# Three pairs of a phase: the 64-row convolution products replaced by a tap on ScalarE and one on VectorE, and a recurrence cut at five eighths

## The chip, the cores and the metric

The kernel runs on one NeuronCore of one Trainium2 chip. The metric is the device time of one execution in microseconds (us), the median of several runs. Engines are named as in the profile: PE (TensorE, the matrix engine), PEld (its weight loads), DVE (VectorE), ACT (ScalarE), POOL (GpSimd) and SP (SyncE, which here only issues DMAs).

## The reference

Four images of 128 channels, 96 x 96. Each is normalised in groups and read as four sequences of 9216 positions (by rows, by columns, and both backwards). Each sequence goes through the same block, and the four results are joined by a 1x1 product and added to the input:

```python
t = grouped1x1(x, in_proj_w, in_proj_b)            # 128 -> 2*256 channels
u, gate = t[:, :256], t[:, 256:]
u = silu(u)
u = depthwise_conv1d(u, dw_w, taps=5)              # along the sequence
s = ssm_in_w @ u                                   # 32 rows
a = 0.999 + 0.0009 * sigmoid(ssm_delta_w @ u + ..) # 32 rows
bb, cc = tanh(ssm_b_w @ u + ..), tanh(ssm_c_w @ u + ..)
h = exp(prefix) * cumsum(bb * s * exp(-prefix))    # h[l] = a[l] * h[l-1] + bb[l] * s[l]
u = u + ssm_out_w @ (cc * h + ssm_d * s)
y = out_proj_w @ grouped1x1(u * sigmoid(gate), mix_w, mix_b)
out = x + fuse_w @ concat(four y) + fuse_b
```

## The kernel before, in words

Everything is float32. The work is cut into 8 phases (4 images, each first in column order, "V", then in row order, "H"; the phases are numbered 0 to 7, V even, H odd). A phase runs two sequences of one image side by side, s = 0 forward and s = 1 backward. It has 6 steps of 1536 positions, and each step is cut into 4 by position modulo 4: the residues p are taken in the order `TURN` = 1, 2, 3, 0. One residue of both sequences is a *pair*; there are 24 pairs in a phase and 192 in all. This text numbers the pairs of a phase as *places* 0 to 23; place modulo 4 gives the pair of the step (0: p = 1, 1: p = 2, 2: p = 3, 3: p = 0).

The 256 channels of `u` lie in two halves of 128. The five taps of the convolution of the second half are made by ACT (tap 0, `first_tap`, L742) and DVE (taps 1 to 4, `taps`, L744). For the first half the channels of four neighbouring positions are spread over 128 rows of the tile `sil`, so that one residue's five taps fall on two column offsets. `conv` multiplies the 128 rows by banded weights (`band`, 4 taps or 3), and what is left lies at the other offset:

- residues 0 and 3 (`alone`): one tap is left. `add_lone` (L691, one DVE instruction) reads that tap's rows, gathered by DMA into `lone`, and adds tap times weight to the product in PSUM while it writes `u`.
- residues 1 and 2: two taps are left, in 64 rows. `conv_less` adds 8 products with weights `less` (64 rows, 32 columns) to the same PSUM bank, and ACT then copies the bank to `u` (`copy_u`, L717).

Up to place 7 and from place 20 on, the pair also computes the input projection of the step ahead (`front`). From place 8 to 19 the front is not needed, since the second half of a phase reads the kept `sil` of the first half backwards; these pairs have the banks (6, 7) of PSUM for `conv`, and most of them make the gates of a later pair instead (`gate`, then `tanh_one` and `tanh_into`, L593 and L599; `tanh_into` reads banks 6 and 7). Steps 2, 3 and 4 (places 8 to 19) are the steps with gates.

A pair in these steps issues on PE, in this order: `conv`, the output product of an older unit (`accumulate`, weights `w_fin`), `conv_less` if it has one, a second `accumulate`, gates (L557) and `out_of` (the ssm output, L577), then `proj` (weights `main`). ACT runs, from the second half of a pair: tanh of two gates (L593), the next pair's tap 0 (L742), tanh of the other two gates from banks 6 and 7 (L599), then what `proj` needs (L781, L784, L790). The recurrence of a whole step, 1536 positions, is one DVE scan cut in two halves of 768 columns (`scan`, L819): part 0 in the first pair of the next step, part 1 in its second pair. The multiplications that use it are on POOL (`outputs`, L825, L826, L828), as are the additions to the output image (`accumulate`, L879).

The program order on each engine is written out by hand; only the semaphores are put in by the framework. SP issues all DMAs in order: the kept gates (L1066, `kept`), kept `sil` tiles (L513), `lone` (L682), gate inputs (L323), input chunks for the statistics of the next image (`xs`, L437, three buffers) and others.

Of the kernel before, what the change touches and what calls it, by code (L numbers as in the profile page):

```python
# [47 lines left out]
P = 128  # L48
# [20 lines left out]
def conv_preact_kernel(  # L69
# [63 lines left out]

    gmeans = wp.tile([P, 2, P], F32, name="gmean")
    gmean = gmeans[:, 0, :]
    per = DIM // GN_GROUPS
# [11 lines left out]
    for e in range(2):  # L148
        nc.gpsimd.tensor_copy(gmeans[:, 1, bass.ts(e, 64)], gmeans[:, 0, bass.ts(1 - e, 64)])
    gmask = wp.tile([P, 4], F32, name="gmask")  # L150
# [25 lines left out]
    def stats_first(b):  # L176
        mv = sp.tile([P, 2], F32, tag="mv", name=f"mv_{b}")
        nc.vector.bn_aggr(mv, stats[b].rearrange("p c s -> p (c s)"))
        yield
        pm = bank(free[0])  # L180
        product(pm[:, 0:1], gmean, mv[:, 0:1])
        mean = sp.tile([P, 1], F32, tag="mean", name=f"mean_{b}")
        nc.vector.tensor_copy(mean, pm[:, 0:1])
        dev = sp.tile([P, 1], F32, tag="dev", name=f"dev_{b}")
        nc.vector.tensor_sub(dev, mv[:, 0:1], mean)
        ex = sp.tile([P, 1], F32, tag="ex", name=f"ex_{b}")
        nc.vector.scalar_tensor_tensor(ex, dev, dev, mv[:, 1:2], ALU.mult, ALU.add)
        gm4 = sp.tile([P, 4], F32, tag="gm4", name=f"gm4_{b}")
        nc.vector.tensor_scalar_mul(gm4, gmask, mean)
        yield  # L190
        pv = bank(free[0])
        for e in range(2):
            product(pv[:, e : e + 1], gmeans[:, e, :], ex)
# [144 lines left out]

    rp = ctx.enter_context(tc.tile_pool(name="shared", bufs=1))

    def shared():
        return rp.tile([P, 16 * P], F32, tag="shared", name="shared")

    b0 = phases[0][0]
# [6 lines left out]
    load_x([(0, 1), (1, 1), (2, 1), (3, 2), (5, 2), (7, 3), (10, 4), (14, 4), (18, 4), (22, 2)])  # L351
    w_out_fuse = shared()
    nc.sync.dma_start(w_out_fuse[:, 0 : 2 * HID + 4 * P], fuse)
# [8 lines left out]
    d_sb, b_mix, b_out, b_fuse = (w_small[:, a:b] for a, b in ((79, 80), (80, 82), (82, 83), (83, 84)))  # L362
    w_edge = w_small[:, 84:86]
    w_out = w_out_fuse[:, 0:HID]
# [8 lines left out]
    def less_of(p):  # L373
        return 1 if p < 2 else 0

    def less_rows(s, p):
# [4 lines left out]
    less = wp.tile([P, R, 4, 32], F32, name="less")  # L381
    w_fin = wp.tile([P, 4, 2, P], F32, name="w_fin")
    b_fin = wp.tile([P, 1], F32, name="b_fin")
    id32 = wp.tile([P, 32], F32, name="id32")
    ident = w_out_fuse[:, 2 * HID + 4 * P : 2 * HID + 5 * P]
# [4 lines left out]
    for s in range(2):  # L390
        for p in range(R):
            for k in range(2):
                r, to = slice(0, P), band[:, s, p]
                if k == less_of(p):
                    r, to = less_rows(s, p), less[:, p]
                m = R * k - p + R - 1
# [34 lines left out]
    def load_chunks(t):  # L431
        ahead = chunks_of(t - 1) + chunks_of(t) + chunks_of(t + 1)
        for b, c in ahead:
            if (b, c) not in loaded and len(chunks) < 3:
                loaded.add((b, c))
                chunks[b, c] = wk.tile([P, SC], F32, tag="xs", bufs=3, name=f"xs_{b}_{c}")
                nc.sync.dma_start(chunks[b, c], xr[b, :, bass.ts(c, SC)])  # L437
# [222 lines left out]
    def alone(p):  # L660
        return p in (0, R - 1)

# [3 lines left out]
    ]  # L666
    lone = {}

# [15 lines left out]
    def add_lone(i, banks):  # L684
# [4 lines left out]
        else:  # L689
# [10 lines left out]
    def conv_less(i, banks, copy=True):  # L700
        step, p = units[i]["step"], units[i]["p"]
        sil, k, b0 = blocks(step), less_of(p), min(banks)
        for g in range(4):
            for s in range(2):
                r = less_rows(s, p)
                mm(bank(b0 + s), g, less[r, p, g, :], columns(step, sil[s][r, g, :], k),
                   False, True)
# [11 lines left out]
    def less_both(i, banks):  # L719
        step, p = units[i]["step"], units[i]["p"]  # L720
        sil, k = blocks(step), less_of(p)
        for g in range(4):
            for s in range(2):
                r = less_rows(s, p)
                mm(bank(banks[s]), g, less[r, p, g, :], columns(step, sil[s][r, g, :], k), False, True)

# [180 lines left out]
    def head_banks(t):  # L907

        return PROJ if t % 2 or t >= LAG else FRONT[1::-1]

    early = [None]

# [42 lines left out]
    def pair_on(t):  # L955
# [3 lines left out]
        un = units[i]  # L959
        single = alone(un["p"])  # L960
        step, g = divmod(t + R, R)
# [27 lines left out]
        taps(i, range(1, K))  # L989
        conv(i, banks, single)  # L990
        if single:
# [57 lines left out]
        if gated is not None:  # L1049
            if gated % NP > 2:  # L1050
                both = to[:, :, 0]
            else:
                spot = 2 - shift
                both = to[:, spot : spot + 2]
            tanh_into(gated, both, 0, psum[:, 6:8, :N])
        if un["order"] == "V" and un["b"] + 1 < B and un["st"] == NS - 1 and k == R - 1:
# [7 lines left out]
        if gated is not None:  # L1064
            if gated % NP > 2:
                nc.sync.dma_start(keep(gated), to)  # L1066
            else:
                nc.sync.dma_start(keep(gated)[:, :, 0], both)
        load_kept(n + 2)
# [307 lines left out]
```

## Time and profile before

| | us |
|---|---|
| median of 3 runs (lowest, highest) | 1737.48 (1737.05, 1737.89) |
| span of the profiled execution | 1735.2 |
| PE busy | 1713.6 (99%) |
| DVE busy | 1507.9 (87%) |
| ACT busy | 1494.8 (86%) |
| POOL busy | 1447.0 (83%) |
| the 64-row products (`less`), busy in all | 84.1, in 96 pairs |

The span runs from the first instruction to the last. The profiled execution's own time is not recorded apart from it; the median lies 2.3 us above the span, which is what lies around it. The granted TensorE clock is 1.000 all through. In rows of the timeline a number is the start in us, the next is how long the group lasted, and brackets tell how long the engine sat idle before it and what ended that. The page counts each float32 product as two MATMUL records.

### The profile page before, as it was taken

How to read it: one execution, taken by the hardware profiler on the slowest of the kernel's cores; microseconds unless marked ns; L12 is line 12 of the kernel's file. 1: busy time of each engine (PE TensorE's matmuls, PEld its weight loads, DVE VectorE, ACT ScalarE, POOL GpSimd, SP SyncE). 2: the span in 40 equal slices, each digit the busy share in tenths (PEclk: the TensorE clock that was granted, in tenths of full speed). 3: DMA queues.
4: the chain of work that ended last, by engine and by line, in shares of the span. 5: the costliest groups of instructions: out<-in, count | busy, mean ns of one | idle time of the engine just before them, and what ended most of it. 6: DMA issues, size and time to landing. Idle time of an engine off the chain costs nothing.

```text
span 1735.2 us, 54226 instructions
## 1 busy us (share of the span) xinstructions
PE 1713.6 (99%) x22522; PEld 644.7 (37%) x22522; DVE 1507.9 (87%) x1508; ACT 1494.8 (86%) x2544; POOL 1447.0 (83%) x1490
## 2 busy tenths in 40 slices
PE   7999999999999999999999999999999999999998
PEld 4333333343333433344333443334333333333333
DVE  6899998888889998888889999888888888888887
ACT  4888988889888888888988888888998889888875
POOL 3689889888789988888788988887878889887887
PEclk9999999999999999999999999999999999999999
DMA  7746865358884786337896487433887548643364
GB/s 244 235 147 218 288 202 151 124 206 280 275 287 139 262 267 194 118 126 263 260 308 226 150 300 251 144 123 132 294 294 239 179 144 304 201 137 133 147 226 166
DMA packets 154644, 363.66 MB, mean 210 GB/s; under 512 B 19104, under 2 KB 120864, under 8 KB 154400
## 3 DMA queue, kind: packets, MB, share of 16 engines
q1 hardware_dynamic: 154256, 360.16, 62.8%
q8 instruction: 178, 2.92, 0.7%
q14 instruction: 66, 0.54, 0.1%
q10 hardware_dynamic: 144, 0.04, 0.0%
HBM read 221.41 MB, written 138.53 MB: 207 GB/s over the span
## 4 chain that ended last, share of the span: by engine, by line
PE 95%; DVE 2%; ACT 1%; DMA 1%; issue 0%; SPq 0%; DVEq 0%; ACTq 0%
PE psum L130 81%; PE psum L577 8%; PE psum L557 5%; DVE psum L744 1%; PE psum L1188 0%; DMA acc<-in_xr 0%; DMA kept<-shared 0%; DVE u L638 0%; ACT psum L589 0%; ACT psum L742 0%; DVE u L744 0%; ACT sil L527 0%; SPq L335 0%; PE psum L1195 0%; DVE u L691 0%
## 5 line engine op out<-in xcount | busy, mean ns | idle before, releaser
L744 DVE SCALAR_TENSOR_TENSOR psum<-sil,small,psum 128x768 f32<-128x768 f32 x576 | 589.1, 1023 | 42.2 <-ACT psum L742 16.8
L130 PE MATMUL psum<-u,w_fin 128*32 128x384 f32 (+1 forms) x6192 | 541.3, 484 | 1.1 <-ACT ys L860 0.4
L130 PE MATMUL psum<-u,main 128*32 128x384 f32 x6144 | 535.0, 489 | 0.5 <-DVE u L691 0.4
L638 DVE SCALAR_TENSOR_TENSOR u<-gate,psum 128x768 f32<-128x768 f32 x376 | 341.7, 950 | 150.0 <-PE psum L577 50.8
L879 POOL TENSOR_TENSOR acc<-ys,acc 128x384 f32<-128x384 f32 x375 | 411.8, 1120 | 14.0 <-ACT ys L860 1.9
L825 POOL TENSOR_TENSOR t<-t,t 64x384 f32<-64x384 f32 (+1 forms) x192 | 287.2, 1496 | 70.6 <-DVE t L819 48.3
L589 ACT COPY psum<-u 128x768 f32<-128x768 f32 x384 | 301.4, 799 | 10.5 <-DVE u L638 4.3
L130 PEld LDWEIGHTS psum<-u,w_fin 128*32 128x32 f32 x6192 | 195.2, 109 | 309.6 <-issue 235.5
L130 PEld LDWEIGHTS psum<-u,main 128*32 128x32 f32 x6144 | 180.0, 109 | 324.5 <-issue 218.3
L130 PE MATMUL psum<-sil,band 128*32 128x384 f32 x3072 | 285.3, 488 | 0.0
L792 POOL TENSOR_SCALAR t<-tm 64x384 f32<-64x384 f32 x184 | 170.8, 928 | 114.4 <-ACT tm L781 102.4
L826 POOL TENSOR_TENSOR t<-t,t 64x384 f32<-64x384 f32 (+1 forms) x192 | 233.9, 1218 | 15.1
L793 POOL TENSOR_TENSOR t<-t,tm 64x384 f32<-64x384 f32 x192 | 213.8, 1113 | 30.2 <-ACT t L784 15.5
L577 PE MATMUL psum<-t,main 32*128 32x384 f32 x1536 | 228.1, 525 | 4.2 <-ACT psum L589 4.2
L742 ACT ACTIVATE psum<-sil,small 128x768 f32<-128x768 f32 x191 | 172.6, 904 | 65.2 <-DVE u L638 61.9
L744 DVE SCALAR_TENSOR_TENSOR u<-sil,small,psum 128x768 f32<-128x768 f32 x192 | 194.9, 1015 | 6.8
L527 ACT ACTIVATE sil<-psum,bnorm 128x385 f32<-128x385 f32 x384 | 191.6, 584 | 4.0 <-DMA edge<-sil 0.9
L557 PE MATMUL psum<-x_in,wn 32*128 32x384 f32 x768 | 161.7, 498 | 0.0
L862 ACT COPY ys<-psum 128x384 f32<-128x384 f32 x288 | 132.3, 478 | 33.0 <-PE psum L130 28.3
L130 PEld LDWEIGHTS psum<-sil,band 128*32 128x32 f32 x3072 | 88.8, 108 | 171.4 <-issue 63.1
L781 ACT ACTIVATE tm<-psum,small 128x384 f32<-128x384 f32 x192 | 110.9, 578 | 14.0 <-PE psum L130 2.3
L577 PEld LDWEIGHTS psum<-t,main 32*128 32x128 f32 x1536 | 93.9, 183 | 73.7 <-issue 41.0
(108 smaller groups left out, 1512.3 us busy)
## 6 DMA issues: line engine op xcount, KB each, us to landing
gate<-kept SPq DMA_DIRECT2D x114, 768.0 KB, 5.2
kept<-gate SPq DMA_DIRECT2D x74, 768.0 KB, 3.7
sil<-sil SPq DMA_DIRECT2D x64, 770.0 KB, 6.6
lone<-edge SPq DMA_DIRECT2D x40, 770.0 KB, 7.5
x_in<-in_xs SPq DMA_DIRECT2D x250, 96.2 KB, 3.3
edge<-sil SPq DMA_DIRECT2D x96, 192.5 KB, 3.6
out<-acc SPq DMA_DIRECT2D x46, 384.0 KB, 6.4
acc<-in_xr SPq DMA_DIRECT2D x39, 384.0 KB, 6.4
```

Of the source, the lines that this page charges most:

```text
L130: nc.tensor.matmul(o[r, : rhs.shape[-1]], lhsT, rhs, start=start, stop=stop, skip_group_check=True)
L527: nc.scalar.activation(sils[step][:, s, j, g, :], bank(bk)[:, : N + 1], AF.Silu, bias=bn[:, 1:2] if j else bn[:, 4 + g : 5 + g],)
L557: nc.tensor.matmul(bank(to)[:, :N], stats[un["b"]][0][r, s, :], x_in[s][r, q, off : off + N], start=True, stop=True)
L577: nc.tensor.matmul(bank(ssm(bi, s) + j)[:, :N], w_so[r, bass.ts(j, P)], z[r, :], start=(bi, s) not in seeded, stop=True, skip_group_check= ...
L589: nc.scalar.copy(psum[:, ssm(bi, s) : ssm(bi, s) + 2, :N], us[bi][:, s])
L638: nc.vector.scalar_tensor_tensor(v, g, 1.0, pz, ALU.add, ALU.mult)
L742: nc.scalar.activation(part, src, AF.Copy, scale=w_tap[:, 0:1])
L744: nc.vector.scalar_tensor_tensor(us[i][:, :, 1, :] if k == K - 1 else part, src, w_tap[:, k : k + 1], part, ALU.mult, ALU.add,)
L793: nc.gpsimd.tensor_mul(ta[0:64, p, :], tb[0:64, :], tm[0:64, :])
L825: engine.tensor_mul(ta[0:64, p, r], tb[64:P, r], ta[64:P, p, r])
L826: engine.tensor_add(tb[0:64, r], ta[0:64, p, r], tb[0:64, r])
L879: adder.tensor_add(part, y, part)
```

## The change

In the second pair of each step with gates (places 9, 13 and 17; `paired`; 24 pairs in all) the 8 products of `conv_less` go. Their two taps are made elsewhere:

- `seed`: one ACT instruction writes tap 1 times its weight into banks 6 and 7 of PSUM, and `conv` adds to it (`onto`) where it used to overwrite. It stands at the end of the pair before (places 8, 12 and 16), right behind `tanh_into`. It reads a new tile, `middle`.
- `add_lone`, as in a pair with one tap left, makes the other tap and writes `u`, so `copy_u` goes too.
- `copy_middle`: `middle` is filled by 8 DMAs per step of 32 rows x 385 columns, issued by SP (`middles`): four in the third pair of the step before, two in its fourth, two in the first pair of the step itself.

The recurrence is cut at 5/8: part 0 has 960 columns, part 1 has 576 (in all steps but the last). To make room in SBUF, `xs` has two buffers for three, `less` holds two residues for four, and `id32` and the second averaging matrix move into the `shared` tile. `less` is no longer built for residues 0 and 3.

On ACT, around places 8 and 9 of phase 0, where `tm_2_1` is the tanh of `proj` at place 8 and `u_2_2` is what place 9 writes. Before:

```order
L742 ACTIVATE psum<-sil_747,small 128x2x384 [waits DVE_49]
L599 ACTIVATE gate_177<-psum,bnorm_272 128x2x384
L781 ACTIVATE tm_2_1_0_1150<-psum,small 128x384 [waits PE_49,Pool_49]
L784 COPY t_0_2_1_0_1133<-psum 64x384 [waits PE_49]
L790 ACTIVATE t_0_2_1_0_1133<-psum,small 64x384
```

After, in the same place (the names' last numbers and the lines differ):

```order
L765 ACTIVATE psum<-sil_740,small 128x2x384 [waits DVE_49]
L604 ACTIVATE gate_172<-psum,bnorm_267 128x2x384
L662 ACTIVATE psum<-middle_897,small 128x2x384 [waits DMAHW5_49,DMAHW6_49,DMAHW4_49,DMAHW7_49,DMAHW3_49,Activation_49]
L804 ACTIVATE tm_2_1_0_1153<-psum,small 128x384 [waits PE_49,Pool_49]
L807 COPY t_0_2_1_0_1136<-psum 64x384 [waits PE_49]
```

The seed (L662) stands between the tanh of banks 6 and 7 and the tanh of `proj`; it waits for the DMAs that fill `middle` and for ACT's own instruction ahead of it.

On PE, from the end of `proj` of place 8 to the gates of place 9, phase 0. Before:

```order
L130 MATMUL psum<-u_2_1_0_1064,main 32x384 x3
L130 MATMUL psum<-u_2_1_0_1064,main 32x384 [waits Activation_49]
L130 MATMUL psum<-u_2_1_0_1064,main 32x384 x7
L130 MATMUL psum<-sil_747,band 32x384 [waits Activation_49]
L130 MATMUL psum<-sil_747,band 32x384 x7
L130 MATMUL psum<-u_0_3_0_577,w_fin 32x384 [waits DVE_49,Activation_49]
L130 MATMUL psum<-u_0_3_0_577,w_fin 32x384 x7
L130 MATMUL psum<-sil_747,less 32x384 x8
L130 MATMUL psum<-u_0_3_0_577,w_fin 32x384 [waits DVE_49,Activation_49]
```

After:

```order
L130 MATMUL psum<-u_2_1_0_1068,main 32x384 x3
L130 MATMUL psum<-u_2_1_0_1068,main 32x384 [waits Activation_49]
L130 MATMUL psum<-u_2_1_0_1068,main 32x384 x7
L130 MATMUL psum<-sil_740,band 32x384 [waits Activation_49]
L130 MATMUL psum<-sil_740,band 32x384 x7
L130 MATMUL psum<-u_0_3_0_572,w_fin 32x384 [waits DVE_49,Activation_49]
L130 MATMUL psum<-u_0_3_0_572,w_fin 32x384 x7
L130 MATMUL psum<-u_0_3_0_572,w_fin 32x384 [waits DVE_49,Activation_49]
```

The 8 `less` products are gone. `conv` (`band`) is still the first thing behind `proj`, and the ACT instruction that its first product waits for is now the seed.

On SP, from place 15 to place 17 of phase 0 (`kept_10` is the gate tile that place 15 made, `sil_17..` the tile of step 5 being loaded back). Before:

```order
L1066 DMA kept_10_188<-gate_176 128x1536
L513 DMA sil_1787<-sil_0_202 128x1540
L513 DMA sil_1787<-sil_1_203 128x1540
L682 DMA lone_1790<-edge_1_211 128x4x385
L437 DMA xs_15_1810<-in_xr 128x384
L323 DMA x_in_70<-in_xs 64x385
L323 DMA x_in_71<-in_xs 64x385
```

After:

```order
L1105 DMA kept_10_183<-gate_171 128x1536
L518 DMA sil_1793<-sil_0_197 128x1540
L518 DMA sil_1793<-sil_1_198 128x1540
L705 DMA lone_1796<-edge_1_206 128x4x385
L687 DMA middle_1609<-sil_442 32x385 x2
L329 DMA x_in_70<-in_xs 64x385
L329 DMA x_in_71<-in_xs 64x385
```

The last two DMAs of `middle` for place 17 stand behind one DMA of 768 KB and three of 770 KB.

The diff, cut to its core:

```diff
+    def paired(t):
+        return 8 <= t % NP < 20 and units[2 * t]["p"] == 2
+
+    def seed(i):
+        step = units[i]["step"]
+        nc.scalar.activation(
+            psum[:, 6:8, :N], columns(step, middle[step], 0), AF.Copy, scale=w_edge[:, 1:2]
+        )
+
-    def conv(i, banks, alone=False):
+    def conv(i, banks, alone=False, onto=False):
...
-                   True, alone)
+                   not onto, alone)
...
+    def copy_middle(step, g):
+        if step % NS not in (2, 3, 4):
+            return
+        if g == 0:
+            middle[step] = wk.tile([P, 2, N + 1], F32, tag="middle", bufs=1, name=f"middle_{step}")
+        for s, q in enumerate((2, R - 1 - 2)):
+            nc.sync.dma_start(
+                middle[step][32 * g : 32 * g + 32, s, :],
+                sils[step][32 * q : 32 * q + 32, s if fresh(step) else 1 - s, 0, g, :],
+            )
...
-            w_edge[:, 1 - k : 2 - k],
+            w_edge[:, 2:3] if p == 2 else w_edge[:, 1 - k : 2 - k],
...
-        r = bass.ts(part, R * N // 2)
+        cut = N // 2 if step == NU // UB - 1 else 5 * N // 8
+        r = slice(R * cut, R * N) if part else slice(0, R * cut)
         if part:
-            init = ta[64:P, R - 1, N // 2 - 1 : N // 2]
+            init = ta[64:P, R - 1, cut - 1 : cut]
...
+    def middles(t):
+        step, k = divmod(t, R)
+        if k == 0:
+            copy_middle(step, R - 1)
+        elif k == 2:
+            copy_middle(step + 1, 0)
+            copy_middle(step + 1, 1)
+        elif k == 3:
+            copy_middle(step + 1, 2)
...
-        single = alone(un["p"])
+        both = paired(t)
+        single = alone(un["p"]) or both
...
         if not fronted:
             under(bi, 1)
+        middles(t)
...
-        conv(i, banks, single)
+        conv(i, banks, single, both)
         if single:
             add_lone(i, banks)
...
             tanh_into(gated, low, 0, psum[:, 6:8, :N])
+        if paired(t + 1):
+            seed(i + 2)
...
-            if (b, c) not in loaded and len(chunks) < 3:
+            if (b, c) not in loaded and len(chunks) < 2:
```

More of the change, by code (lines that the diff above doesn't have):

```diff
@@ L131, in mm, with shared @@
                          skip_group_check=True)
-    gmeans = wp.tile([P, 2, P], F32, name="gmean")
-    gmean = gmeans[:, 0, :]
+    rp = ctx.enter_context(tc.tile_pool(name="shared", bufs=1))
+    def shared():
+        return rp.tile([P, 16 * P], F32, tag="shared", name="shared")
+    w_out_fuse = shared()
+    gmean = wp.tile([P, P], F32, name="gmean")
+    gmeans = (gmean, w_out_fuse[:, 15 * P : 16 * P])
     per = DIM // GN_GROUPS
@@ L192, in stats_first @@
         for e in range(2):
-            product(pv[:, e : e + 1], gmeans[:, e, :], ex)
+            product(pv[:, e : e + 1], gmeans[e], ex)
         var = sp.tile([P, 2], F32, tag="var", name=f"var_{b}")
@@ L362, in conv_preact_kernel @@
     d_sb, b_mix, b_out, b_fuse = (w_small[:, a:b] for a, b in ((79, 80), (80, 82), (82, 83), (83, 84)))
-    w_edge = w_small[:, 84:86]
+    w_edge = w_small[:, 84:87]
     w_out = w_out_fuse[:, 0:HID]
@@ L374, in less_of, with alone @@
         return 1 if p < 2 else 0
+    def alone(p):
+        return p in (0, R - 1)
     def less_rows(s, p):
@@ L380, in conv_preact_kernel @@
     band = wp.tile([P, 2, R, 4, 32], F32, name="band")
-    less = wp.tile([P, R, 4, 32], F32, name="less")
+    less = wp.tile([P, 2, 4, 32], F32, name="less")
     w_fin = wp.tile([P, 4, 2, P], F32, name="w_fin")
     b_fin = wp.tile([P, 1], F32, name="b_fin")
-    id32 = wp.tile([P, 32], F32, name="id32")
+    id32 = w_out_fuse[:, 13 * P : 13 * P + 32]
     ident = w_out_fuse[:, 2 * HID + 4 * P : 2 * HID + 5 * P]
@@ L394, in conv_preact_kernel @@
                 if k == less_of(p):
-                    r, to = less_rows(s, p), less[:, p]
+                    if alone(p):
+                        continue
+                    r, to = less_rows(s, p), less[:, p - 1]
                 m = R * k - p + R - 1
@@ L666, in conv_preact_kernel @@
     ]
-    lone = {}
+    lone, middle = {}, {}
+    def copy_middle(step, g):
[8 more added lines that the diff above has]
+            )
     def edge_of(step):
@@ L705, in conv_less @@
                 r = less_rows(s, p)
-                mm(bank(b0 + s), g, less[r, p, g, :], columns(step, sil[s][r, g, :], k),
+                mm(bank(b0 + s), g, less[r, p - 1, g, :], columns(step, sil[s][r, g, :], k),
                    False, True)
@@ L724, in less_both @@
                 r = less_rows(s, p)
-                mm(bank(banks[s]), g, less[r, p, g, :], columns(step, sil[s][r, g, :], k), False, True)
+                mm(bank(banks[s]), g, less[r, p - 1, g, :], columns(step, sil[s][r, g, :], k), False, True)
     def new_u(i):
@@ L1050, in pair_on @@
             if gated % NP > 2:
-                both = to[:, :, 0]
+                low = to[:, :, 0]
             else:
                 spot = 2 - shift
-                both = to[:, spot : spot + 2]
-            tanh_into(gated, both, 0, psum[:, 6:8, :N])
+                low = to[:, spot : spot + 2]
+            tanh_into(gated, low, 0, psum[:, 6:8, :N])
+        if paired(t + 1):
+            seed(i + 2)
         if un["order"] == "V" and un["b"] + 1 < B and un["st"] == NS - 1 and k == R - 1:
@@ L1067, in pair_on @@
             else:
-                nc.sync.dma_start(keep(gated)[:, :, 0], both)
+                nc.sync.dma_start(keep(gated)[:, :, 0], low)
         load_kept(n + 2)
@@ L1338 @@
         v["fuse_b"],
-        v["dw_w"].reshape(HID, K)[:P, [K - 1, 0]],
+        v["dw_w"].reshape(HID, K)[:P, [K - 1, 0, 1]],
     ]
```

10 lines of the change are left out of this document (2 added, 8 removed).

## The prediction

> **What bounds the kernel now.** I read the page first: busy shares and the chain that ended last.
>
> ```profile
> PE 1713.6 (99%) x22522; PEld 644.7 (37%) x22522; DVE 1507.9 (87%) x1508; ACT 1494.8 (86%) x2544; POOL 1447.0 (83%) x1490
> ...
> PE 95%; DVE 2%; ACT 1%; DMA 1%; issue 0%; SPq 0%; DVEq 0%; ACTq 0%
> ```
>
> PE is the bound: it is busy all the time, and 95% of the chain lies on it. So I read the price of a product from the pace of PE, in the timeline of PE alone, at places 8 to 10 of phase 1; `conv` (`band`) opens each pair.
>
> ```profile
> 299.89 1.48 PE L130 MATMUL psum<-sil,band 128*32 128x384 f32 x16
> ...
> 309.00 1.47 PE L130 MATMUL psum<-sil,band 128*32 128x384 f32 x16
> ...
> 318.12 1.47 PE L130 MATMUL psum<-sil,band 128*32 128x384 f32 x16
> ...
> 326.38 0.83 PE L130 MATMUL psum<-sil,band 128*32 128x384 f32 x8
> ```
>
> Places 8 and 9 take 9.11 and 9.12 us, place 10, which has no `less`, 8.26. A pair without `less` is 0.86 shorter, and 24 of them would give 24 x 0.86 = 20.6 us. That is the naive sum. It holds if nothing new stops PE, so the next view is ACT, which gets the new instruction ahead of `conv`. The timeline of ACT at the end of place 8:
>
> ```profile
> 306.97 0.90 ACT L742 ACTIVATE psum<-sil,small 128x768 f32<-128x768 f32 x1
> 307.80 0.89 ACT L599 ACTIVATE gate<-psum,bnorm 128x768 f32<-128x768 f32 x1
> ```
>
> The tanh that reads banks 6 and 7 (L599) ends at 308.69, and `conv` of place 9 writes these banks at 309.00. Only 0.31 us lie between, and the seed has to fit there.
>
> **The seed, step by step.** It has the shape of L742 (768 columns, SBUF to PSUM), so 0.90 us. The order shows that it waits for ACT's own instruction ahead. The nearest row with such a wait is the first copy to PSUM behind a silu that read the same bank, on ACT in a pair with a front; the restart of PE after ACT is seen once, at place 19 of phase 2:
>
> ```profile
> 229.77 2.00 ACT L527 ACTIVATE sil<-psum,bnorm 128x385 f32<-128x385 f32 x4
> 231.80 1.53 ACT L589 COPY psum<-u 128x768 f32<-128x768 f32 x2
> ```
>
> ```profile
> 615.14 0.90 ACT L599 ACTIVATE shared<-psum,bnorm 128x768 f32<-128x768 f32 x1 [0.89 <-DMA kept<-shared]
> ...
> 616.09 1.05 PE L130 MATMUL psum<-x_in,wn 32*32 32x385 f32 x32 [0.59 <-ACT shared L599]
> ```
>
> The copy starts 0.03 after the silu ends (231.77), where L599 starts 0.07 before L742 ends. PE goes on 0.05 after ACT's end (616.04). So the seed would run 308.72 to 309.62 and `conv` start at 309.67, 0.67 late. Restarting with an empty pipe costs something more; no row isolates it for `conv`, so I estimate 0.05, ends 0 and 0.10. Of the 0.86 saved, 0.86 - 0.72 = 0.14 is left here.
>
> **The longer part 0 of the scan** stands ahead of this chain at the same places, since tap 0 (L742) waits for the first of the two gatings (L638), and that stands behind the scan on DVE. The timeline of DVE, at place 12 of phase 0 and places 8 and 12 of phase 1:
>
> ```profile
> 126.47 3.08 DVE L819 TENSOR_TENSOR_SCAN t<-t,t 64x768 f32<-64x768 f32 x1
> 129.57 1.82 DVE L638 SCALAR_TENSOR_TENSOR u<-gate,psum 128x768 f32<-128x768 f32 x2
> ...
> 303.54 1.81 DVE L819 TENSOR_TENSOR_SCAN t<-t,t 64x768 f32<-64x768 f32 x1
> 305.91 1.82 DVE L638 SCALAR_TENSOR_TENSOR u<-gate,psum 128x768 f32<-128x768 f32 x2 [0.56 <-ACT ys L862]
> ...
> 337.82 2.67 DVE L819 TENSOR_TENSOR_SCAN t<-t,t 64x768 f32<-64x768 f32 x1
> 340.67 1.82 DVE L638 SCALAR_TENSOR_TENSOR u<-gate,psum 128x768 f32<-128x768 f32 x2 [0.17 <-PE psum L577]
> ```
>
> 768 columns take 1.81 when nothing is in the way; the longer records hold a wait. 960 columns in proportion take 2.26, 0.45 more; with a fixed part it is less, and I take 0.42. At place 8 of an H phase DVE idles 0.56 before L638: no effect. At place 12 of an H phase it idles 0.17: L638 comes 0.25 later, L742 (behind L593 on ACT already) 0.20. In a V phase L638 follows the scan at once, so all 0.42 goes on to ACT:
>
> ```profile
> 130.57 0.91 ACT L742 ACTIVATE psum<-sil,small 128x768 f32<-128x768 f32 x1
> 131.41 0.88 ACT L599 ACTIVATE gate<-psum,bnorm 128x768 f32<-128x768 f32 x1
> ```
>
> ```profile
> 132.39 1.47 PE L130 MATMUL psum<-sil,band 128*32 128x384 f32 x16
> ```
>
> L599 ends 0.42 later, at 132.71, the seed at 133.64, and `conv` of place 13 starts at 133.69 and not at 132.39: 1.30 late, 1.35 with the restart. That is more than the 0.86 saved; the two pairs lose 0.49.
>
> **The copies into `middle`.** At place 16 SP sends back kept `sil` tiles, and the last two copies stand behind them. SP at place 16 of phases 1 and 6; what the issues of those moments took to land (last number); and when `conv` of place 17 starts on PE:
>
> ```profile
> 369.59 1.32 SPq L513 DMA_DIRECT2D sil<-sil  x2
> 371.00 0.44 SPq L682 DMA_DIRECT2D lone<-edge  x1
> 371.54 1.30 SPq L323 DMA_DIRECT2D x_in<-in_xs  x2
> ...
> 1428.17 0.45 SPq L682 DMA_DIRECT2D lone<-edge  x1
> ```
>
> ```profile
> lone<-edge SPq DMA_DIRECT2D x1, 770.0 KB, 8.4
> x_in<-in_xs SPq DMA_DIRECT2D x1, 96.2 KB, 8.3
> ...
> lone<-edge SPq DMA_DIRECT2D x1, 770.0 KB, 10.3
> ```
>
> ```profile
> 378.49 1.47 PE L130 MATMUL psum<-sil,band 128*32 128x384 f32 x16
> ...
> 1435.65 1.48 PE L130 MATMUL psum<-sil,band 128*32 128x384 f32 x16
> ```
>
> In phase 1 `lone` lands at 379.40 and the small DMA behind it at 379.84; the new copies stand between them, and I take 379.65. `conv` of place 17 has started by then (378.49), so the seed, which has to come first, waits for a DMA: it would run 379.70 to 380.60 and `conv` start at 380.65, 2.16 late. With the restart and the saving the two pairs lose 2.16 + 0.05 - 0.86 = 1.35. In phase 6 `lone` lands at 1438.47; with the copies at 1438.70 `conv` starts at 1439.70, 4.05 late, and the loss is 3.24. I read no landing in the other phases and reckon six like phase 1 and two like phase 6: mean 1.82. ACT waits for the DMA with all that `proj` needs behind the seed (L781, L784, L790), and so do POOL's products from them; PE stands at `conv` and needs none of it sooner.
>
> At place 12 nothing large stands ahead of the copies, and at place 8 `lone` alone; I charge nothing there.
>
> [...]
>
> **What else moves.** `copy_u` leaves ACT in the second pair: nothing, since ACT there waits for PE. `add_lone` comes on DVE, one more instruction of 128x768 (1.0, like L744's), and part 1 of the scan is 0.42 shorter: DVE gets 0.6 more. I cost it nothing, because `conv`, and with it all of PE, is 0.7 or more late in that pair, while DVE's taps are not; if that cover is gone, L638 comes late and `conv` of the third pair after it (rival D). The longer part 0 in pairs with a front: nothing, by the slack of place 8 in phase 1 (0.56); if it is gone, L742 is late there. Two `xs` buffers make SP wait for the statistics of the same pair, with a whole pair (8.26) until the next use: nothing, or DVE waits. 192 small DMAs on SP's queue: nothing but the wait above, or loads behind them come some tenths later. The moved tiles and the shorter building of `less` lie in the start, behind the loads.
>
> **The sum.** Place 8, H: 4 x -0.14 = -0.6. Place 8, V: the scan there lies between the two kinds shown; I take half way from -0.14 to 0.49, rounded up for the larger loads, +0.3 each, +1.2. Place 12, H: 0.67 + 0.20 + 0.05 - 0.86 = +0.06, x 4 = +0.2. Place 12, V: 4 x 0.49 = +2.0. Place 16: 8 x 1.82 = +14.6. Together +17.4. The profiled span of 1735.2 becomes 1752.6; the median of the runs lies 2.3 above the span, so 1754.9.
>
> **Rivals.** (A) is the forecast: slower, 1754.9. With all eight phases like phase 1, place 16 costs 10.8 and the time is 1751; with all like phase 6, 25.9 and 1766. Chance 0.64.
>
> (B) The copies land before L599 ends. Then place 16 is like place 12, 4 x 0.49 + 4 x 0.06 = 2.2, the sum is +5.0 and the time 1742.5. With the restart at 0 instead of 0.05 in 24 places it is +3.8, and a little less elsewhere brings it under 3.5, the 0.2% that a measurement of this kernel can just tell from no change. Chance 0.20, half of it within 0.2%.
>
> (C) On the other side: the seed is hidden. If it ended by 309.06, say because ACT runs it ahead of L599's end or the gates are ready sooner, `conv` would start as now, all 24 pairs fall to 8.26, and the time is 1737.5 - 20.6 = 1716.9. It decides where the seed takes no longer than the 0.31 between L599 and `conv`; the row of its shape has 0.90. For it speaks that ACT is idle 14% of the time, against it that ACT's rows here follow each other without a gap. Chance 0.08.
>
> (D) DVE becomes late in the second pair: `add_lone` pushes part 1 of the scan into POOL's addition, and L638, L742, L599 and the third pair's `conv` follow; an estimated 0.3 in each of 12 V pairs adds 3.6 to A, 1758.5. Chance 0.08.
>
> **How the numbers follow.** The likeliest is A, 1754.9. The range 1741 to 1762 holds A but for the worst landings, D, and the half of B above 0.2%; C, the other half of B (0.18 together) and A's upper edge stay outside, some 0.2. Faster is C, 0.08; within 0.2% half of B, 0.10; slower A, D and the rest of B, 0.82.
>
> **What would show it.** In the timeline of the changed kernel: PE idle ahead of `conv` at places 9, 13 and 17, released by the ACT seed, some 0.7 at place 9 of an H phase, 1.3 at place 13 of a V phase and 2 or more at place 17; ACT idle ahead of the seed at place 16, ended by the DMA of `middle`; second pairs at 8.3; scans of about 2.2 and 1.4 where nothing holds them. I am wrong if the seed at place 16 starts right behind L599, if `conv` starts before the seed's end, or if pairs 9, 13 and 17 last longer than 8.4.

## The result, and the profile after

The changed kernel takes 1797.96 us (median of four runs, 1795.30 to 1801.04) where the kernel before takes 1737.43 on the same chip: 1.035 times as long, 95% interval 1.033 to 1.036. The forecast was 1754.9. Slower was right, but the loss is 60.5 us and not 17.4.

The page of the changed kernel, the lines that answer to those of before: busy shares, the chain that ended last by engine, and by line.

```profile
PE 1719.8 (96%) x22138; PEld 653.7 (36%) x22138; DVE 1526.6 (85%) x1532; ACT 1498.8 (83%) x2544; POOL 1450.6 (81%) x1486
...
PE 80%; DVE 6%; DMA 6%; ACT 5%; issue 2%; SPq 1%; ACTq 0%; DVEq 0%
PE psum L130 68%; PE psum L582 7%; PE psum L562 5%; DMA middle<-sil 3%; DVE psum L767 3%; DMA x_in<-in_xs 2%; DVE t L843 1%; ACT psum L662 1%; DVE u L643 1%; ACT psum L765 1%; ACT gate L604 1%; DVE u L767 1%; ACT psum L594 0%; DMA acc<-in_xr 0%; ACT gate L598 0%
```

PE has 192 products fewer (384 records, two for each product) and is busy 6 us longer: some products run slower than before. PE's part of the chain fell from 95% to 80%. The waits of the same kernel (in total, times, longest):

```profile
PE psum L130 <- ACT psum L662: 52.2, 24, 4.8
...
ACT psum L662 <- DMA middle<-sil: 19.7, 7, 3.8
...
ACT psum L662 <- DMA x_in<-in_xs: 12.7, 4, 4.1
```

All 24 second pairs wait for the seed (L662), 52.2 us together. 11 of the 24 seeds wait for the copies into `middle`, 32.4 us together; the four rows that name `x_in` are such waits too, as the place below shows. One such place in full: PE at place 16 of phase 1 (the last products of the pair, then `conv` of place 17), SP and ACT there, and the resources in stretches (stretch, its length, busy time and instructions of five engines, granted clock, DMA share, GB/s).

```profile
389.32 2.79 PE L130 MATMUL psum<-u,main 128*32 128x384 f32 x32
396.84 2.74 PE L130 MATMUL psum<-sil,band 128*32 128x384 f32 x16 [4.73 <-ACT psum L662]
399.33 3.28 PE L130 MATMUL psum<-u,w_fin 128*32 128x384 f32 x32
```

```profile
384.44 0.45 SPq L705 DMA_DIRECT2D lone<-edge  x1
384.94 1.35 SPq L687 DMA_DIRECT2D middle<-sil  x2
```

```profile
390.93 0.88 ACT L604 ACTIVATE gate<-psum,bnorm 128x768 f32<-128x768 f32 x1
395.88 0.90 ACT L662 ACTIVATE psum<-middle,small 128x768 f32<-128x768 f32 x1 [4.07 <-DMA x_in<-in_xs]
```

```profile
387.70:392.10 4.40, 4.40 (x52) 1.74 (x48) 4.22 (x5) 3.37 (x5) 4.18 (x4) 1.00 1.01 389
392.10:396.80 4.70, 0.00 (x1) 0.00 (x0) 3.05 (x3) 0.92 (x2) 1.89 (x2) 1.00 1.06 353
396.80:400.20 3.40, 3.36 (x24) 1.25 (x28) 0.52 (x1) 2.73 (x5) 1.90 (x2) 0.52 0.72 301
400.20:403.60 3.40, 3.40 (x42) 1.69 (x36) 1.91 (x2) 1.77 (x4) 1.30 (x2) 0.98 0.02 7
```

The DMA engines are full from 387.7 to 396.8; the copies stand behind `lone` and the loads ahead of it. The seed starts 4.07 after the tanh (the row names `x_in`, which was issued right behind the copies and landed with them). Then comes what the prediction did not hold at all: after 4.73 us of standing still, the 8 products of `conv` (16 records) take 2.74 and not 1.47, and the granted clock is 0.52 over the next 3.4 us.

Against the trace of before, `conv` to `conv`, summed over the eight phases:

| places | change, us | predicted |
|---|---|---|
| 8 and 9 | +13.4 | +0.6 |
| 12 and 13 | +2.5 | +2.2 |
| 16 and 17 | +40.3 | +14.6 |
| 22 and 23, phase 0 alone | +5.4 | 0 |
| all others | -0.1 | 0 |

The last row is +0.32 at place 5 of phase 0, -0.5 at place 19, +0.17 and -0.17 at two places 10 and hundredths elsewhere. The spans differ by 62.0; what the table lacks of that lies ahead of the first `conv` and in the last pair.

### The profile page after: what moved, and what is told of

Read it like the earlier page. It is cut to its first block, busy times and chain, and to the rows that moved or that the text cites. A ratio compares the mean times of both kernels' runs of the same rounds, so it can differ in the third digit from the quotient of the medians.

```text
span 1797.2 us, 53786 instructions
## 1 busy us (share of the span) xinstructions
PE 1719.8 (96%) x22138; PEld 653.7 (36%) x22138; DVE 1526.6 (85%) x1532; ACT 1498.8 (83%) x2544; POOL 1450.6 (81%) x1486
## 4 chain that ended last, share of the span: by engine, by line
PE 80%; DVE 6%; DMA 6%; ACT 5%; issue 2%; SPq 1%; ACTq 0%; DVEq 0%
PE psum L130 68%; PE psum L582 7%; PE psum L562 5%; DMA middle<-sil 3%; DVE psum L767 3%; DMA x_in<-in_xs 2%; DVE t L843 1%; ACT psum L662 1%; DVE u L643 1%; ACT psum L765 1%; ACT gate L604 1%; DVE u L767 1%; ACT psum L594 0%; DMA acc<-in_xr 0%; ACT gate L598 0%
## 5 line engine op out<-in xcount | busy, mean ns | idle before, releaser
L849 POOL TENSOR_TENSOR t<-t,t 64x384 f32<-64x384 f32 (+1 forms) x192 | 304.8, 1588 | 81.6 <-DVE t L843 63.8
L130 PE MATMUL psum<-sil,band 128*32 128x384 f32 x3072 | 297.2, 505 | 52.2 <-ACT psum L662 52.2
L130 PEld LDWEIGHTS psum<-u,w_fin 128*32 128x32 f32 x6192 | 200.9, 111 | 315.2 <-issue 252.5
L594 ACT COPY psum<-u 128x768 f32<-128x768 f32 x384 | 301.4, 800 | 10.5 <-DVE u L643 4.3
L850 POOL TENSOR_TENSOR t<-t,t 64x384 f32<-64x384 f32 (+1 forms) x192 | 232.5, 1211 | 15.1
L582 PE MATMUL psum<-t,main 32*128 32x384 f32 x1536 | 223.1, 524 | 4.4 <-ACT psum L594 4.4
L816 POOL TENSOR_TENSOR t<-t,tm 64x384 f32<-64x384 f32 x192 | 199.6, 1039 | 29.3 <-ACT t L807 14.5
L714 DVE SCALAR_TENSOR_TENSOR u<-lone,small,psum 128x768 f32<-128x768 f32 x120 | 121.1, 1009 | 36.5 <-PE psum L130 36.5
L598 ACT ACTIVATE gate<-psum,bnorm 128x384 f32<-128x384 f32 x152 | 87.8, 580 | 41.7 <-PE psum L562 31.0
```

The lines of the kernel that those rows point to most:

```text
L130: nc.tensor.matmul(o[r, : rhs.shape[-1]], lhsT, rhs, start=start, stop=stop, skip_group_check=True)
L582: nc.tensor.matmul(bank(ssm(bi, s) + j)[:, :N], w_so[r, bass.ts(j, P)], z[r, :], start=(bi, s) not in seeded, stop=True, skip_group_check= ...
L594: nc.scalar.copy(psum[:, ssm(bi, s) : ssm(bi, s) + 2, :N], us[bi][:, s])
L816: nc.gpsimd.tensor_mul(ta[0:64, p, :], tb[0:64, :], tm[0:64, :])
L849: engine.tensor_mul(ta[0:64, p, r], tb[64:P, r], ta[64:P, p, r])
L850: engine.tensor_add(tb[0:64, r], ta[0:64, p, r], tb[0:64, r])
```

## The experiments

Theory: three things stand beside the seed's own time. Copies come late (places 8 and 16), PE runs at half pace after long stalls (second pairs; 2.74 for 1.47 above), and with two `xs` buffers DVE waits once. Rivals: traffic or DVE makes these pairs long, whatever the seed waits for.

**Two `xs` buffers alone** (`xs_two`), on the kernel before.

```
-            if (b, c) not in loaded and len(chunks) < 3:
+            if (b, c) not in loaded and len(chunks) < 2:
-  chunks[b, c] = wk.tile([P, SC], F32, tag="xs", bufs=3, ...)
+  chunks[b, c] = wk.tile([P, SC], F32, tag="xs", bufs=2, ...)
```

> The kernel before with two xs buffers in place of three, nothing else. Theory (the third chunk of pair 22 of phase 0 has to wait until the statistics of the same pair free a buffer, and DVE stands with it): one stall of some 3.7 us at place 22 and 1.6 in the pair behind it, as in the changed kernel, so 1737.4 + 5.4 = 1743. Rival (that stall comes from the other edits, since the loads have a whole pair): 1737.4.

Measured: 1742.96, ratio 1.0036 [1.0023, 1.0049]. DVE at place 22 of phase 0 in this kernel:

```profile
215.68 1.01 DVE L445 BATCH_NORM_STATS2 bn<-xs 128x6 f32<-128x384 f32 x2
220.77 0.56 DVE L445 BATCH_NORM_STATS2 bn<-xs 128x6 f32<-128x384 f32 x1 [4.08 <-DMA xs<-in_xr]
221.25 1.80 DVE L638 SCALAR_TENSOR_TENSOR u<-gate,psum 128x768 f32<-128x768 f32 x2
```

Three chunks belong to this pair. The third can only be loaded when the statistics of the first have freed a buffer, and the gating (L638) stands behind it on DVE. Places 22 and 23 are 3.9 and 2.5 longer, no other place but for -0.7 at one. The theory holds; the 2.5 at place 23 is the clock again, which is 0.50 from 223.03 to 226.44 (last section); `conv` takes 2.79 there and the 32 records of `w_fin` behind it 4.11, where `split` has 1.50 and 2.76 below.

**The cut of the recurrence alone** (`scan_only`), on the kernel before.

```
-        r = bass.ts(part, R * N // 2)
+        cut = N // 2 if step == NU // UB - 1 else 5 * N // 8
+        r = slice(R * cut, R * N) if part else slice(0, R * cut)
-            init = ta[64:P, R - 1, N // 2 - 1 : N // 2]
+            init = ta[64:P, R - 1, cut - 1 : cut]
```

> The kernel before with the recurrence cut at five eighths, nothing else. Theory: where the seed does not stand ahead of the convolution, 0.31 us of slack take most of the 0.42 that part 0 grows by; 0.1 us at about eight places of V phases, 1738.3 (1737.4 to 1739). Rival (the longer part 0 is dear by itself, because it collides with POOL): 8 x 4 steps with 0.4 each, about 1750.

Measured: 1741.32, ratio 1.0029 [1.0018, 1.0040]; by the spans of the traces +3.5. The expectation was too small: it took the 0.31 us of slack that place 8 of an H phase has. Place 12 of phase 0 in this kernel, DVE and PE:

```profile
127.35 3.48 DVE L820 TENSOR_TENSOR_SCAN t<-t,t 64x960 f32<-64x960 f32 x1
```

```profile
133.63 1.50 PE L130 MATMUL psum<-sil,band 128*32 128x384 f32 x16 [0.17 <-ACT gate L599]
```

Part 0 takes 3.48 where it took 3.08, and PE waits for L599. V phases lose 0.33 to 0.39 at places 12 and 16 and 0.10 to 0.30 at place 8, H phases nothing; place 5 of phase 0 loses 0.32, as in the changed kernel. The rival's 0.4 in every step, H phases too, did not happen.

**The seed without a wait for its data** (`seed_ready`), on the changed kernel.

```
-  psum[:, 6:8, :N], columns(step, middle[step], 0), AF.Copy, ...
+  psum[:, 6:8, :N], columns(step, sils[step][:, :, 1, 0, :], 0), AF.Copy, ...
```

> The changed kernel, the seed reading a slice of the sil tile that has long been there in place of middle (the tap is wrong); the copies into middle are still made. Theory (the seed waits for the copies, and PE's clock falls after the long stalls): place 16 falls to the 10.4 and 10.0 of place 12 (-24.6 over eight phases), place 8 of three V phases to 10.4 (-6.9), the second pairs behind them to 8.34 (-17.4), together 1797.9 - 48.9 = 1749. Rival (the traffic of those moments or DVE makes these pairs long, not the wait): over 1780.

Measured: 1748.27, ratio 1.0066 [1.0051, 1.0081], where 1749 was expected. The copies are still made, so their traffic is there; the wait alone is gone. Place 16 falls to 9.78 to 10.43, place 8 to 9.79 to 10.39, all second pairs to 8.34 to 8.39 but the last, which takes 7.70. From the changed kernel's trace to this one, places 8 and 16 lose 32.6 us and places 9 and 17 lose 18.0. So 50.6 of the 62.0 come from late copies. Against the kernel before, the six places still cost 5.5: that is the seed and the cut by themselves.

**Idle products in the stall** (`fill`, then `fill_free`), on the changed kernel. The first stood ahead of `conv` and wrote bank 6:

```
+        if both and t % NP == 17:
+            for _ in range(24):
+                for g in range(4):
+                    nc.tensor.matmul(psum[32 * g : 32 * g + 32, 6, 400:512], band[:, 0, 0, g, :], ...)
         conv(i, banks, single, both)
```

> The changed kernel with 96 idle products of 112 columns ahead of the convolution of place 17, an estimated 2.6 us on PE while it would stand still; they write columns that nothing reads. The seed's wait stays. Theory (clock: after a stall of over 2.5 us PE runs at half pace for some 3 us): place 16 keeps its 11.8 to 14.1, place 17 falls from 9.4 to 10.8 to 8.4 in all phases, -11 to -12.5 together, 1786. Rival (place 17 is long because operands come late from DVE, ACT or DMA): no change, 1798, or more by what the products push back.

Measured: 1830.24, ratio 1.0542 [1.0520, 1.0563]. The edit missed its aim: the products write a bank that the seed writes, so they waited for it too, and took 7.14 and not 2.6. (The 2.6 was too small by itself: 44 such products take 2.29 in the next run, so 96 would take an estimated 5.0.) PE at place 17 of phase 0:

```profile
172.89 7.14 PE L1030 MATMUL psum<-sil,band 128*32 128x112 f32 x192 [4.49 <-ACT psum L662]
179.86 1.46 PE L130 MATMUL psum<-sil,band 128*32 128x384 f32 x16
```

It tells one thing: `conv` behind them runs at full pace. But its operands had 7 us more to arrive, so this does not part the theories. The second stood behind the projection and wrote bank 2:

```
         proj(i, PROJ, not fronted)
+        if paired(t + 1) and t % NP == 16:
+            for _ in range(11):
+                for g in range(4):
+                    nc.tensor.matmul(psum[32 * g : 32 * g + 32, 2, 400:512], band[:, 0, 0, g, :], ...)
```

> The changed kernel with 44 idle products of 112 columns behind the projection of place 16, in columns of bank 2 that nothing reads; unlike those of the run before (which stood behind the seed) they run while PE waits for the seed, by the 7.14 us that 96 of them took an estimated 2.4 us. The seed's wait stays. Theory (clock: after a stall of over 2.5 us PE runs at half pace): place 16 stays at 11.8 to 14.1, place 17 falls to 8.4 in all phases, 1797.9 - 12.5 = 1786. Rival (operands come late in place 17): 1798.

Measured: 1780.86, ratio 1.0258 [1.0234, 1.0282]: 17 us faster than the changed kernel by doing more work. PE at place 16 of phase 0:

```profile
166.68 2.79 PE L130 MATMUL psum<-u,main 128*32 128x384 f32 x32
169.28 2.29 PE L1117 MATMUL psum<-u,band 128*32 128x112 f32 x88
173.70 1.50 PE L130 MATMUL psum<-sil,band 128*32 128x384 f32 x16 [2.13 <-ACT psum L662]
```

The seed comes as late as ever (place 16 lasts 11.88 to 13.78), but PE stands still for 2.13 only, and place 17 lasts 8.34 in phases 0 to 6 and 7.70 in the last, where the changed kernel has 9.89 to 10.78 in six of the seven and 9.40. That gives back 13.2 us. The rest lies at place 16 (2.0), places 22 and 23 (1.8) and places 8 and 9 (0.8); that it is scatter of the landings alone is not shown. `conv` behind this stall takes 1.50, where the changed kernel has 2.79 at a granted clock of 0.50 (171.67 to 178.50). Operands that came late would have come as late here.

**The copies one pair earlier** (`early_xs`), on the changed kernel; the chunk plan is changed so that no pair has three.

```
-  places = singles[2:] * 2 + [LAG - 1, NP - 4, NP - 3, NP - 2]
+  places = singles[2:] * 2 + [LAG - 1, NP - 4, NP - 3, NP - 3]
-        if k == 0:
-            copy_middle(step, R - 1)
-        elif k == 2:
+        if k == 2:
             copy_middle(step + 1, 0)
             copy_middle(step + 1, 1)
         elif k == 3:
             copy_middle(step + 1, 2)
+            copy_middle(step + 1, R - 1)
```

> The changed kernel with the last two copies into middle issued one pair earlier, with those before them (the data is there), and with the chunks of pair 22 of phase 0 spread so that two buffers do. Theory (all that is over the seed's own 0.9 us comes from late copies, the clock after them, and xs): as with the seed on data that is there, less the xs stall, 1748.3 - 6.9 = 1741.4 (1740 to 1743). Rival (192 small transfers push back other loads wherever they stand): over 1748.

Measured: 1743.27, ratio 1.0039 [1.0026, 1.0053]. That is 5.3 over the kernel before of its series, where the changed kernel was 60.5 over. Its profiled run was the slowest of its five (span 1747.0); in that trace places 9 to 13 of phases 2 and 6 are 6.1 longer than with ready data. No seed waits for a copy there. What the trace shows is that the four copies now stand right ahead of the `acc` loads on SP (511.04 to 514.60 in phase 2, `acc` from 514.64), that POOL's additions wait 3.8 and 4.6 for landings in these two phases (at most 1.0 for `acc` in the kernel before), and that POOL is still late at place 12, where in phase 6 the scan waits 1.05 for it. That the copies cause it follows from this order; no run parts it.

**The cut at one half again** (`half`), on `early_xs`.

```
-        cut = N // 2 if step == NU // UB - 1 else 5 * N // 8
+        cut = N // 2
```

> The kernel early_xs with the recurrence cut at one half again. Theory (the longer part 0 stands ahead of the seed's chain in V phases, and part 1 has 0.49 us of idle time ahead of the gating in the second pair, measured with the seed on ready data): 12 V places 0.34 shorter, second pairs as they are, 1743.3 - 4.1 = 1739. Rival (DVE needs the shorter part 1 in the second pair): second pairs up to 0.4 longer in 24 places, 1747 to 1749.

Measured: 1739.65, ratio 1.0019 [1.0010, 1.0028], where 1739 was expected. Place 12 of phase 0 falls from 10.39 to 10.04, the second pairs stay at 8.34 in most phases. With the seed in its place, DVE does not need the shorter part 1.

What is left is the seed. Three runs ask whether its 0.9 us can be hidden.

**Bank by bank** (`split`), on `early_xs`: the seed as two instructions of 384 columns.

```
-        nc.scalar.activation(
-            psum[:, 6:8, :N], columns(step, middle[step], 0), ...
+        for s in range(2):
+            nc.scalar.activation(
+                psum[:, 6 + s, :N], columns(step, middle[step][:, s], 0), ...
```

> The kernel early_xs with the seed in two instructions of 384 columns, bank 6 first. Theory (the convolution starts as soon as its first bank is seeded): by the row of a 128x384 ACT instruction, 0.56, PE starts 0.34 earlier in 24 pairs, 1741.4 - 8.2 = 1733. Rival (the second half, 0.56 too, stops the convolution halfway, or PE waits for both): 1741 or a little over.

Measured: 1744.41, ratio 1.0040 [1.0019, 1.0061], the time that the rival gave, but not for its reason. `conv` starts 0.3 sooner (place 8 of phase 1: 9.47 for 9.79), and the second pair takes 8.70 for 8.34. PE at place 9 of phase 1:

```profile
311.62 1.50 PE L130 MATMUL psum<-sil,band 128*32 128x384 f32 x16 [0.18 <-ACT psum L663]
312.94 2.76 PE L130 MATMUL psum<-u,w_fin 128*32 128x384 f32 x32
...
316.22 0.96 PE L582 MATMUL psum<-t,main 32*128 32x384 f32 x8
```

The second half of the seed does not stop `conv`: what stands behind it starts 1.32 later, as in `early_xs`. It gives the time back on ACT. The two halves take 1.09 where the whole seed takes 0.90, and what `out_of` (L582) needs of ACT follows them there without a gap, up to the copy L594. So `out_of` starts 4.60 after `conv` and not 4.24, and what the start wins is gone.

**Ahead of tap 0** (`swap`), on `early_xs`.

```
-        first_tap(i + 2)
+        if not paired(t + 1):
+            first_tap(i + 2)
...
         if paired(t + 1):
             seed(i + 2)
+            first_tap(i + 2)
```

> The kernel early_xs with tap 0 (ACT) put behind the seed at places 8, 12 and 16, so that tanh of banks 6 and 7 and the seed run 0.9 us earlier and tap 0 1.8 us later. Theory (the loss is the seed's place in the ACT chain ahead of the convolution, and DVE can take its taps later): the convolution starts as before the change and the second pairs keep their 0.78, so 1736.6 - 18.5 = 1718, up to 1724 with small waits. Rival (DVE is nearly full in the second pair, 8.4 us of work in 8.3, so a late tap 0 comes back as a late first gating and a late convolution one pair later, 0.5 to 0.9 in 24 places): 1732 to 1742.

Measured: 1764.21, ratio 1.0153 [1.0137, 1.0168]: worse than the rival. `conv` is on time everywhere (first pairs 9.11 but for one), but the second pairs take 10.0 (22 of 24, one 10.6, the last 9.3), and the third pairs 0.17 more. DVE, ACT and PE in the second pair, place 13 of phase 1:

```profile
349.74 3.14 DVE L767 SCALAR_TENSOR_TENSOR psum<-sil,small,psum 128x768 f32<-128x768 f32 x3 [1.66 <-ACT psum L765]
352.91 1.01 DVE L767 SCALAR_TENSOR_TENSOR u<-sil,small,psum 128x768 f32<-128x768 f32 x1
...
356.33 1.82 DVE L643 SCALAR_TENSOR_TENSOR u<-gate,psum 128x768 f32<-128x768 f32 x2
```

```profile
353.96 0.80 ACT L594 COPY psum<-u 128x768 f32<-128x768 f32 x1 [0.96 <-DVE u L767]
```

```profile
354.90 0.94 PE L582 MATMUL psum<-t,main 32*128 32x384 f32 x8 [0.93 <-ACT psum L594]
```

Tap 0 comes 1.66 late, the last tap frees its banks late, the copy into them (L594), the products behind it (L582) and the gating follow in turn. This loop has no room in the second pair: its delay comes back whole.

**No seed at all** (`no_seed`), on `early_xs`.

```
-        if paired(t + 1):
-            seed(i + 2)
...
-        conv(i, banks, single, both)
+        conv(i, banks, single, False)
```

> The kernel early_xs without the seed: tap 1 of the 64 rows is left out, the convolution starts its banks itself, all else stays (copies into middle, addition of lone, cut at five eighths). Naive (each second pair 0.78 to 0.86 shorter, nothing in its place): 1737.4 - 20.6 = 1717. Theory (without the seed the second pair is bound by the loop over DVE: four taps 4.16, addition 1.01, part 1 of the recurrence 1.42, gatings 1.82, some 0.2 of handing over, 8.6 us, where PE needs 8.26; V phases keep 0.34 for the longer part 0): 1737.4 - 24 x 0.5 + 12 x 0.34 = 1729.

Measured: 1734.22, ratio 0.9985 [0.9974, 0.9996]. DVE through the second pair and into the third (places 13 and 14 of phase 1):

```profile
343.13 3.14 DVE L767 SCALAR_TENSOR_TENSOR psum<-sil,small,psum 128x768 f32<-128x768 f32 x3
346.30 1.01 DVE L767 SCALAR_TENSOR_TENSOR u<-sil,small,psum 128x768 f32<-128x768 f32 x1
347.23 1.01 DVE L714 SCALAR_TENSOR_TENSOR u<-lone,small,psum 128x768 f32<-128x768 f32 x1
348.27 1.42 DVE L843 TENSOR_TENSOR_SCAN t<-t 64x576 f32<-64x576 f32 x1
349.72 1.82 DVE L643 SCALAR_TENSOR_TENSOR u<-gate,psum 128x768 f32<-128x768 f32 x2
351.65 3.14 DVE L767 SCALAR_TENSOR_TENSOR psum<-sil,small,psum 128x768 f32<-128x768 f32 x3
```

There is no gap on DVE: 8.52 from the first tap of one pair to that of the next. The second pair takes 8.46 there (before 9.11), the third 0.17 more than before; in most V pairs it is 8.7, with 0.35 more in the first pair. So even a free seed would win 3 us with these copies and this cut, and not 20.6. The expectation of 1729 had 0.5 less for each of 24 pairs; H phases reach it (0.65 less 0.17), V phases do not (0.41 less 0.17), and phases 2 and 6 lose some 3 us more at places 9 and 12, as in `early_xs`.

No version that does the whole work beats the kernel before; the nearest, `half`, is 1.0019 times as long.

## Why the prediction was wrong

**What held.** The seed ahead of `conv` on ACT's serial chain. The row of place 12 of phase 0 shows it as worked out:

```profile
133.00 0.88 ACT L604 ACTIVATE gate<-psum,bnorm 128x768 f32<-128x768 f32 x1
133.92 0.91 ACT L662 ACTIVATE psum<-middle,small 128x768 f32<-128x768 f32 x1
```

The start gap is 0.04 (predicted 0.03), and `conv` follows 0.05 after the seed's end. Place 12 lasts 10.40 to 10.43 in V and 9.97 to 9.99 in H phases, place 13 lasts 8.34: the term of +2.2 measured +2.5. Place 8 of H phases: 9.80 and 8.34 make 18.14 for 18.23, -0.09 for -0.14. Place 8 of phase 0, where nothing was late, has +0.48 with its second pair for +0.3. Rival C's idle time of ACT was of no use, as the forecast said; DVE (rival D) did not come late in these pairs because `conv` was late itself, and `swap` and `no_seed` show that it is the next bound.

**What failed, the largest first.** The four terms below make 18.0, 12.3, 7.6 and 5.4, 43.3 together, where the loss is 43.1 over the forecast.

*The pace of PE behind a stall.* The prediction took every product at its full pace and a restart at 0.05; it said that second pairs over 8.4 would prove it wrong. They last up to 10.78. The only term that it had for this, 0.05 for the restart, was an estimate, and no run shows it: behind 14 of the 24 seeds `w_fin` starts 1.31 or 1.32 after `conv`, where the kernel before has 1.29 or 1.30 at these places, so some 0.02, and behind the other 10 the pair is 1.5 to 2.4 longer. The clock after stalls costs 18.0 us at places 9 and 17 (`seed_ready` against the changed kernel), and some 1.6 at place 23 of phase 0 (counted with the `xs` buffers below). `fill_free` shows the cause. This was a step left out, not one mis-sized: long stalls were predicted for place 17 (2.16 to 4.05 late), and what PE does after one was not asked.

*The copies at place 16,* estimated to make `conv` 2.16 late in six phases and 4.05 in two, a mean of 2.63. It was 2.69 to 5.03 late, a mean of 4.16 (33.3 in all and not 21.0). The mis-sized number is a landing read at two places: `lone`, which the copies follow, took 8.4 us at this place of phase 1 in the trace of before, and 10.9 in that of the changed kernel (8.5 to 10.9 over its phases). The landings scatter, since in `fill_free` the same place is 2.15 shorter; most phases were like the worse of the two that I read, not like the better.

*The copies at place 8,* charged with nothing because `lone` alone stood ahead. Wrong for three V phases, +7.6 in waits. The queue was not read there. SP in phase 2 shows 1.5 MB of `acc` and two chunks of `xs` going out in the 4.5 us ahead of `lone` and the copies:

```profile
529.42 2.95 SPq L1021 DMA_DIRECT2D acc<-in_xr  x4
532.48 0.89 SPq L442 DMA_DIRECT2D xs<-in_xr  x2
533.42 0.42 SPq L705 DMA_DIRECT2D lone<-edge  x1
533.89 1.73 SPq L687 DMA_DIRECT2D middle<-sil  x2
```

*The two `xs` buffers,* "nothing, or DVE waits". It was the second: 5.4 in the changed kernel, and 6.5 in the trace of `xs_two`. The condition named (a whole pair until the next use) does not hold where one pair has three chunks, which the code of the chunk plan shows.

The chance of rival B (copies in time, 1742.5) was 0.20. The run that makes it true, `early_xs` (which also takes the `xs` stall out), has 1743.3, and the six places of `seed_ready` cost 5.5 for B's 5.0: the sum behind B was sound, the landings were not.

From issue to landing, the last two copies at place 16 took 8.0 to 10.6 over the phases; in phase 1 (10.0 and 10.6) the DMA engines were full (a share of 1.01 and 1.06 above). The least of all 192 copies is 1.9.

```profile
DMA to landing us min/median/max: 1.9/3.3/10.6
```

## What to carry to other kernels

Price an added wait twice: the time that it takes, and the pace of PE after it; stalls of PE of 2.5 us and more mostly cost 1.5 to 2.4 us more in the pair behind them here, and a few idle products in the stall paid for themselves. Before a small transfer is put where an engine at the bound will wait for it, add up what its queue carries ahead of it at every such place, not at one; one pair earlier made these copies nearly free. And when work is taken off the engine at the bound, ask what the next loop needs: here DVE, with the tap that it was given, had 8.5 us of its own for a pair of 9.1, so 0.6 was all that there was to win, and the replacement cost more.

## What the runs showed of the hardware

Behind ten of the 24 stalls of PE that a seed ends, the granted clock is 0.50 in the trace of the changed kernel. The first products after stalls of 2.50 and 2.62 us (four records of the same `conv`):

```profile
1493.44 0.53 PE L130 MATMUL psum<-sil,band 128*32 128x384 f32 x4 [2.50 <-ACT psum L662]
...
834.12 0.87 PE L130 MATMUL psum<-sil,band 128*32 128x384 f32 x4 [2.62 <-ACT psum L662]
```

In this trace `conv` is at full pace after 2.50 and less (1.50 for its 16 records); after the ten stalls of 2.62 to 4.85 it runs at half pace from its start or from a point within (1.83 to 2.79), and the pair is 1.54 to 2.44 longer, whatever the length of the stall (4.54: 2.43, 4.73: 1.69). That looks like a sharp limit, and it is none: in `xs_two` PE has the clock at 0.50 behind a stall of 2.46.

Here are stretches around four stalls. Those of phase 0 (the first four rows) and phase 3 (the next two) are cut where the clock changes, the two of phase 6 lie around the stall of 2.50, as those of phase 3 a whole number of their lengths behind the first fall, and the last two rows are of `xs_two`, cut at its own fall. The first number behind the length is how long PE was busy, the one before the last two is the granted clock.

```profile
168.26:171.67 3.41, 0.77 (x12) 0.08 (x4) 3.21 (x4) 0.87 (x2) 3.27 (x4) 1.00 1.04 324
171.67:175.08 3.41, 1.51 (x12) 0.59 (x16) 0.87 (x1) 2.42 (x5) 0.91 (x2) 0.50 1.01 368
175.08:178.50 3.42, 3.42 (x24) 0.98 (x20) 1.99 (x2) 1.23 (x2) 1.00 (x1) 0.50 0.44 178
178.50:181.91 3.41, 3.41 (x40) 1.66 (x36) 1.08 (x2) 2.26 (x5) 2.75 (x3) 1.00 0.00 0
830.44:833.86 3.42, 1.06 (x16) 0.17 (x8) 3.31 (x4) 1.46 (x2) 2.80 (x4) 1.00 1.07 349
833.86:837.27 3.41, 3.15 (x20) 0.99 (x24) 0.98 (x2) 2.95 (x6) 1.91 (x2) 0.50 0.99 379
1489.22:1492.63 3.41, 1.72 (x24) 0.44 (x16) 3.23 (x5) 1.87 (x3) 3.19 (x5) 1.00 1.08 355
1492.63:1496.04 3.41, 2.60 (x32) 1.06 (x36) 2.75 (x3) 3.36 (x6) 2.88 (x3) 1.00 1.00 332
...
219.62:223.03 3.41, 1.02 (x20) 0.18 (x16) 2.26 (x3) 0.81 (x1) 1.72 (x2) 1.00 0.41 135
223.03:226.44 3.41, 3.34 (x28) 0.82 (x32) 3.20 (x5) 3.36 (x8) 2.11 (x5) 0.50 0.63 224
```

In phase 0 the clock falls at 171.67, while PE stands still (`conv` comes at 173.57), and is back at 178.50; in phase 3 it is 0.50 from 833.86 to 837.27. In these rows PE is busy for 0.77, 1.06 and 1.02 of the stretch ahead of a fall; the stall of 2.50 lies across two stretches, PE is busy for 1.72 and 2.60 of them, and the clock is 1.00 in both. That this parts them everywhere is not shown. The half clock lasts 6.83 us in phases 0 and 5, whose pairs lose 2.4, and 3.41 behind the other eight stalls, which lose 1.5 to 1.7.

One kind of fall stays open. In `half` and `no_seed`, `conv` at place 6 of phase 0 takes 2.64 and 2.53 for its 16 records, and 1.50 at places 5 and 7, though the rows of PE at place 5 leave no gap but one of 0.25 us in `no_seed`; place 6 takes 0.4 us more there.
